# Selective scans of four directions on one core: a second buffer for x, one PSUM evacuation per projection, sums of y in column quarters, and more zero products on TensorE

## The chip, the cores and the metric

The kernel runs on one core of a Trainium2 chip. The metric is the device time of one execution in microseconds. The engines are named as the profile names them: PE is TensorE (matmuls), PEld its weight loads, DVE is VectorE, ACT is ScalarE, POOL is GpSimd, and SP is the queue that issues most DMAs.

## What is computed

A network of four layers on four images of 64 x 64 tokens with 96 channels. Layers 0 and 1 each run a selective scan in four directions over 4096 tokens, 192 inner channels and 16 states; layers 2 and 3 are an attention, a Fourier layer and feed-forward parts. The change lies in the scans, which both layers share:

```python
dts = jnp.einsum('bkrl,kdr->bkdl', dts, dt_projs_weight)
delta = jax.nn.softplus(dts + dt_projs_bias...)
def step(h, inp):
    dt, u, Bl, Cl = inp
    h = h * jnp.exp(dt[..., None] * A) + (dt * u)[..., None] * Bl[:, :, None, :]
    y = jnp.einsum('bkdn,bkn->bkd', h, Cl)
    return (h, y)
_, ys = jax.lax.scan(step, h0, (dt_t, u_t, B_t, C_t))
```

Layer 0's directions 0 and 1 follow the diagonals in a snake, 2 and 3 go by radius; layer 1's go along rows and columns, forwards and backwards. Afterwards the four results are put back in token order and added up.

## The kernel before

All is float32 in the scans. `Stream.run` (L1342) takes eight batches, one for each layer and image. Each is 4 directions x 4 segments of 1024 tokens, 16 segments in a row. Between two batches stands `side_by_side` (L748), which finishes the batch before (`merge`) and prepares the next image (`front`: input projection, convolution, x in token order in DRAM). Its small tiles (z_rows, xc, y_rows, yt, dx, halo) have buffers of their own.

**A segment** (`batch`, L1184) is 24 groups: 6 blocks of 32 channels (cb) by 4 blocks of 4 states (sg), so a group has 128 partitions (channel, state) and 1024 columns (tokens). For each group
- ACT makes the decay exp(dt*A) (`decay`, L1072),
- DVE makes t = u * B from PSUM (`enter`, L1076) and scans it (`recur`, L1083),
- POOL multiplies the states with C (`leave`, L1098), into a ring of three tiles hc,
- PE adds up the four states of each channel (`collect`, L1107): a product with the 128 x 32 matrix gather_y, summed in PSUM over the four groups of a channel block.

For each channel block PE first spreads dt*u over the states (`spread_u`, L1065) into the one PSUM tile u. DVE's order is fixed: enter, enter, recur, recur for each pair of groups. Two channel blocks make a pair: `collect` writes its 1024 tokens as two products of 512 columns, into two of the four 32-row quarters of the one PSUM bank y; once the pair is whole, `copy_y` (L1136) copies the bank, `turn` (L1148) transposes it, `keep_rows` (L1152) puts it into rows, and `store` (L1154) sends these to DRAM: for layer 0's directions 0 and 1 eight indirect scatters that POOL issues, otherwise one or two DMAs of SP.

**The next segment** is prepared meanwhile (`prepare`, L871): `turn_x` (L897) transposes its x, `keep_x` copies it to the one tile xs, `project` (L934) makes dt (192 channels, in two halves) and B and C for two halves of the tokens each, and `split` (L938) evacuates each projection: |dt + bias| and relu(dt + bias), with B and C in the first half. `low` (L986) and `log` work out softplus in four terms (with what exp loses in a low part), `add` (L1014) sums the terms on PE with the identity, `keep_dt` copies them, `times` (L1023) makes dt*u on POOL and so reads xs last. All PSUM steps but y, u and t share one bank, "m".

**The order** of all instructions of a batch is written by a planner, `Flow.run` (L136): each `Op` has an engine, a cost (`occ`), a latency to other engines, a due time and the operations it needs; "hard" ones (DVE, decay, leave, spread) may not be put off by others. Each engine works its queue in the order given. At each plan gap on PE, `keep_busy` (L1117) adds products with zeros (L1125: 96 x 32 zeros times 256 columns), which leave the sums as they are, but only where a group's sum is open in y:

```python
for _ in range(int((gap - 0.15) * 0.7 / 0.215)):
    self.nc.tensor.matmul(gr.seg.y[at : at + GC, :256], self.zeros, ..., start=False, stop=False, ...)
```

`self.open` is the last group collected, or None behind a block's fourth. The plan's costs are 0.87 for a collect, 1.75 for a spread, 0.88 and 0.87 for a product of `project` and `add`, 0.55 for `turn_x` and 0.5 for `turn`; a pair of groups takes 6.74 on DVE.

Of the kernel before, what the change touches and what calls it, by code (L numbers as in the profile page):

```python
# [113 lines left out]
class Op:  # L114


    def __init__(self, engine, occ, emit, deps=(), lat=0.15, due=None, hard=False, bank=0, after=0.0):
        self.engine, self.occ, self.emit, self.lat = engine, occ, emit, lat
        self.deps = [d for d in deps if d is not None]
        self.due, self.hard, self.bank, self.after = due, hard, bank, after  # L120
        self.users, self.left, self.seen = [], 0, 0.0


class Flow:
# [11 lines left out]
    def run(self):  # L136
# [22 lines left out]
        while left:  # L159
            best = None  # L160
            for engine, ops in ready.items():
# [7 lines left out]
                if strict and first:  # L169
                    limit = first[-1].due + drift - (3.2 if engine == "PE" else 0.5)  # L170
# [20 lines left out]
            if engine == "PE":  # L191
                self.fill(start - free[engine])
# [4 lines left out]
            free[engine] = start + op.occ  # L197
            done = start + op.occ
# [4 lines left out]
            for user in op.users:  # L203
                user.seen = max(user.seen, done if user.engine == engine else done + op.lat)
# [100 lines left out]
class Layer:  # L305


    def __init__(self, s, a, pre, x_in):
# [24 lines left out]
        self.bias_bc = None  # L333
        if self.ordered:
            self.bias_bc = k.t(w, [128, ND], pre + "dir_bc")
            nc.sync.dma_start(self.bias_bc[C:], a[pre + "dirBC"])
        conv_w = k.load(s.seg, a[pre + "conv_w"], "conv_w")
# [39 lines left out]
class Stream:  # L377
# [4 lines left out]
    def __init__(self, k, ctx, a, x, x1, y1):  # L382
# [20 lines left out]
        self.bc = k.t(w, [128, 2, NSG, SEG], "bc")  # L403
        self.zeros = k.t(w, [C, GC], "zeros")
        nc.gpsimd.memset(self.zeros, 0.0)

# [5 lines left out]
    def front(self, bt, plan, rings, first=None):  # L412
# [22 lines left out]
        def edges(s, st):  # L435

            halo = yield from take(self.tmp, [C, 2, HW], "halo", 2)
# [29 lines left out]
        def project(s, st):  # L467
# [31 lines left out]
            def outer(j):  # L499
# [6 lines left out]
                z = yield from take(self.tmp, [C, 2, CH], "z_rows", 2)  # L506
# [19 lines left out]
        def convolve(s, st):  # L526
            yield lambda: st.pad is not None
            xc = []
            for _ in range(C // GC):
                xc.append((yield from take(self.tmp, [128, CH], "xc", 3)))  # L530
# [26 lines left out]
            rows = yield from take(self.tmp, [128, 2, 4, DI], "y_rows", 1)  # L557
# [27 lines left out]
    def merge(self, bt, plan, rings):  # L585
# [29 lines left out]
        def times_d(n):  # L615

            x = yield from take(tmp, [128, T, DI], "dx", 1)
# [73 lines left out]
        def finish(n, acc, mv):  # L691
# [20 lines left out]
            yt = yield from take(tmp, [C, 2, CH], "yt", 1)  # L712
# [35 lines left out]
    def side_by_side(self, ahead, behind=None, flush=None, seg=None):  # L748
# [3 lines left out]
        plan, rings = Plan(), Rings(k)  # L752
        self.ended, self.idle = False, None
# [117 lines left out]
    def prepare(self, seg, base=0.0, before=None):  # L871
# [7 lines left out]
        def op(name, engine, occ, emit, deps=(), at=0.0, **kw):  # L879
            x = Op(engine, occ, emit, deps, due=base + at, **kw)  # L880
# [22 lines left out]
        def keep_x(j, parts):  # L903
            if (j, parts[0]) == (0, 0):
                seg.xs = k.t(self.seg, [C, 2, SEG], "xs")
# [9 lines left out]
        for j in range(0, SEG // 128, 2):  # L915
            here = [f for n, f in enumerate(seg.fetched) if len(seg.fetched) < 4 or seg.turned or n // 2 == j // 2]
            here.append(o.get(("X", j - 2)))
            if j == 0:
                here += [b.get(("u", h)) for h in range(2)]
# [18 lines left out]
        def split(half, j, what):  # L938
            if (half, j, what) == (0, 0, 0):
# [6 lines left out]
            if what == 0:  # L946
                nc.scalar.activation(v.z[:, half, cols], ps[:C], AF.Abs, bias=bias)  # L947
            elif what == 1:
                nc.scalar.activation(v.dt[:, half, cols], ps[:C], AF.Relu, bias=bias)
            elif lay.bias_bc is None:  # L950
                nc.scalar.copy(v.bc[:, cols], ps[C:])
            else:
                nc.scalar.activation(v.bc[:, cols], ps[C:], AF.Identity, bias=lay.bias_bc[C:, kd : kd + 1])

        last, chain = o["xs", SEG // 128 - 2], None
        for half in range(2):
            for j in range(2):
                at = 20.0 + 3.5 * (2 * half + j)
                free = []
                if (half, j) == (0, 0):  # L960
                    free = [b.get(n) for n in (("u", 0), ("u", 1), ("out", 0), ("out", 1), "bc_out", ("sum", 1, 1))]
# [13 lines left out]
                p = op(("z", half, j), "ACT", 0.6, partial(split, half, j, 0), [p], at=at + 2.0)  # L975
                if half == 0:
                    p = op(("z", half, j), "ACT", 0.63, partial(split, half, j, 2), [p], at=at + 3.0)
                op(("z", half, j), "ACT", 0.65, partial(split, half, j, 1), [p], at=at + 4.0, bank=-1)
# [7 lines left out]
        def low(half, what):  # L986
            if (half, what) == (0, 0):
                seg.dtu = k.t(self.seg, [C, 2, SEG], "dtu", bufs=2)
            z, r = v.z, seg.dtu
            if what == 0:  # L990
                nc.scalar.activation(z[:, half], z[:, half], AF.Exp, scale=-1.0)
            elif what == 1:
# [5 lines left out]
        for half in range(2):  # L998
            p = op(("low", half, 0), "ACT", 1.08, partial(low, half, 0), [o["z", half, 1], p], at=32.0 + 5.0 * half)
            p = op(("low", half, 1), "ACT", 1.08, partial(low, half, 1), [p], at=33.5 + 5.0 * half)  # L1000
            p = op(("low", half, 2), "ACT", 1.08, partial(low, half, 2), [p], at=35.0 + 5.0 * half)
# [6 lines left out]
        op("log", "ACT", 4.6, log, [o["low", 0, 2], o["low", 1, 2], b.get(("sum", 1, 1))], at=42.0)  # L1008
# [91 lines left out]
    def collect(self, gr):  # L1100

        nc, seg, cb = self.nc, gr.seg, gr.cb
        if gr.sg == 0 and cb % 2 == 0:
            seg.y = self.k.t(self.ps_y, [128, CH], "y")
        for part in range(2):
            at = (part * 2 + cb % 2) * GC
            nc.tensor.matmul(  # L1107
                seg.y[at : at + GC, :],
                self.gather_y,
                gr.hc[:, part * CH : (part + 1) * CH],  # L1110
# [4 lines left out]
        self.open = gr if gr.sg < NSG - 1 else None  # L1115

    def keep_busy(self, gap):  # L1117


        gr = self.open  # L1120
        if gr is None:
            return
        at = gr.cb % 2 * GC
        for _ in range(int((gap - 0.15) * 0.7 / 0.215)):
            self.nc.tensor.matmul(  # L1125
                gr.seg.y[at : at + GC, :256],
                self.zeros,
                gr.seg.bt.lay.diag.rearrange("p h t c -> p (h t c)")[:, :256],
                start=False,
                stop=False,  # L1130
# [1257 lines left out]
```

## Time and profile before

| | us |
|---|---|
| three runs | 15387.51, 15395.76, 15419.16 |
| median | 15395.76 |
| the profiled execution | 15402.95 |
| its span | 15401.2 |
| scan batches, first to last scan: layer 0 | 1350, 1331, 1338, 1326 |
| layer 1 | 1303, 1294, 1301, 1295 |
| between two batches | 99 to 225 |
| behind the last batch (layer 1's feed-forward, layers 2 and 3) | 3207 |
| granted TensorE clock, mean | 0.937 |

| engine | busy us | share of the span |
|---|---|---|
| PE | 13827.4 | 90% |
| DVE | 12827.4 | 83% |
| POOL | 9203.3 | 60% |
| ACT | 8327.7 | 54% |

| group of instructions | count | mean ns |
|---|---|---|
| recur, DVE L1083 | 3072 | 2355 and 2287 |
| enter, DVE L1076 | 3072 | 1239 |
| leave, POOL L1098 | 3072 | 2365 |
| dt*u, POOL L1023 | 256 | 2356 |
| decay, ACT L1072 | 3072 | 1151 |
| Abs and Relu in split, ACT L947, L949 | 512 each | 684, 679 |
| collect, PE L1107 | 12288 | 620 |
| zero products, PE L1125 | 7824 | 386 |

A matmul's duration runs to its modelled end, and matmuls overlap, so the time that one takes in the stream is the distance between starts. PE's 90% holds the zero products too. A product in float32 stands as two instructions.

### The profile page before, as it was taken

The numbers are of one execution on the slowest core, as the hardware profiler recorded it, in microseconds if no ns is written. First come the engines' busy times: TensorE is split into PE (matmuls) and PEld (weight loads), VectorE is DVE, ScalarE is ACT, GpSimd is POOL, SyncE is SP. The second block draws the span as 40 slices with busy tenths as digits, with TensorE's granted clock in tenths as the row PEclk, the third lists the DMA queues.
The fourth block names the chain that finished last, engine by engine and source line by source line (L and its number), as shares of the span: only waits on it lengthen the run. The fifth ranks groups of instructions, "written<-read, shape, count | busy, mean of one in ns | idle before, by whom it ended". The sixth has DMA issues, their size and how long they took to land. (4 is left out here: it accounts for less than half of the span.)

```text
span 15401.2 us, 196660 instructions
## 1 busy us (share of the span) xinstructions
PE 13827.4 (90%) x74369; PEld 5096.1 (33%) x74369; DVE 12827.4 (83%) x9642; ACT 8327.7 (54%) x13421; POOL 9203.3 (60%) x4657
## 2 busy tenths in 40 slices
PE   8899899989998999899989998999899789998877
PEld 3233333333333333333333333333233244443344
DVE  1999799978997899799979997999899856555655
ACT  3666466646664666466656665666566423232333
POOL 0788678867886688667747774777577620000123
PEclk9999899989998999899989999999999999998888
DMA  2333433343334333433343334333433400000122
GB/s 67 117 113 125 150 111 111 126 148 112 111 127 146 106 118 128 148 116 117 123 152 124 118 124 152 126 118 120 156 119 120 142 10 11 19 15 12 52 72 71
DMA packets 662768, 1637.49 MB, mean 106 GB/s; under 512 B 102822, under 2 KB 268460, under 8 KB 658045
## 3 DMA queue, kind: packets, MB, share of 16 engines
q1 hardware_dynamic: 624956, 1549.37, 31.4%
q0 software_dynamic: 36864, 75.55, 1.7%
q8 instruction: 588, 9.63, 0.3%
q14 instruction: 360, 2.94, 0.1%
HBM read 1295.03 MB, written 329.58 MB: 105 GB/s over the span
## 5 line engine op out<-in xcount | busy, mean ns | idle before, releaser
L1098 POOL TENSOR_TENSOR hc<-h,bc 128x1024 f32<-128x1024 f32 x3072 | 7198.4, 2365 | 2216.1 <-DVE h L1083 1909.0
L1083 DVE TENSOR_TENSOR_SCAN h<-da,state,t 128x1024 f32<-128x1024 f32 x2304 | 5300.4, 2355 | 26.0 <-ACT state L1094 16.3
L1072 ACT ACTIVATE da<-dts,L_A_logs 128x1024 f32<-128x1024 f32 x3072 | 3520.0, 1151 | 1832.2 <-DVE h L1083 1786.7
L1076 DVE TENSOR_TENSOR t<-u,bc 128x1024 f32<-128x1024 f32 x3072 | 3629.8, 1239 | 267.6 <-PE u L1065 193.5
L1107 PE MATMUL y<-hc,gather_y 128*32 128x512 f32 x12288 | 3529.1, 620 | 311.9 <-POOL hc L1098 241.7
L1125 PE MATMUL y<-L_diag,zeros 96*32 96x256 f32 x7824 | 1986.3, 386 | 0.0
L1083 DVE TENSOR_TENSOR_SCAN h<-da,t 128x1024 f32<-128x1024 f32 x768 | 1717.4, 2287 | 17.3 <-ACT da L1072 9.1
L1065 PE MATMUL u<-dtu,spread 32*128 32x512 f32 x3072 | 1573.1, 632 | 120.0 <-DVE t L1076 109.2
L1125 PEld LDWEIGHTS y<-L_diag,zeros 96*32 96x32 f32 x7824 | 852.8, 111 | 1425.0 <-issue 926.1
L1107 PEld LDWEIGHTS y<-hc,gather_y 128*32 128x32 f32 x12288 | 595.8, 109 | 2021.1 <-issue 1029.1
L934 PE MATMUL m<-xs,proj 96*128 96x512 f32 (+1 forms) x2048 | 1070.2, 641 | 67.3 <-ACT spare L1152 32.5
L1642 DVE SCALAR_TENSOR_TENSOR hcv<-padv,taps,hcv 128x2048 f32<-128x2048 f32 x384 | 902.2, 2350 | 13.4
L1566 POOL MEMSET padp<- 128x2448 f32 x32 | 68.6, 2143 | 1400.8 <-PE d L1606 1378.3
L1023 POOL TENSOR_TENSOR dtu<-dt,xs 96x1024 f32<-96x1024 f32 x256 | 603.0, 2356 | 506.1 <-ACT dt L1017 501.1
L1606 PE MATMUL d<-padp,diag 32*32 32x512 f32 x25600 | 885.7, 601 | 2.0 <-ACT hcp L1621 2.0
L1065 PEld LDWEIGHTS u<-dtu,spread 32*128 32x128 f32 x3072 | 521.4, 188 | 943.6 <-issue 588.0
L1017 ACT COPY dt<-m 96x512 f32<-96x512 f32 x512 | 297.2, 580 | 694.5 <-PE m L1014 690.0
L1014 PE MATMUL m<-dtu,ident 96*96 96x512 f32 x1024 | 563.8, 632 | 72.7 <-ACT dt L1017 65.9
L1606 PEld LDWEIGHTS d<-padp,diag 32*32 32x32 f32 x25600 | 484.4, 103 | 369.8 <-issue 196.9
L934 PEld LDWEIGHTS m<-xs,proj 96*128 96x128 f32 (+1 forms) x2048 | 324.6, 181 | 770.6 <-issue 483.8
L947 ACT ACTIVATE sp_z<-m,L_dtb 96x512 f32<-96x512 f32 x512 | 350.0, 684 | 409.5 <-PE m L934 393.5
L1014 PE MATMUL m<-sp_log,ident 96*96 96x512 f32 x1024 | 539.2, 608 | 0.0
(275 smaller groups left out, 15495.8 us busy)
## 6 DMA issues: line engine op xcount, KB each, us to landing
bc<-bc_dram SPq DMA_DIRECT2D x1024, 512.0 KB
dts<-dt_dram SPq DMA_DIRECT2D x768, 512.0 KB
dt_dram<-dt SPq DMA_DIRECT2D x256, 384.0 KB
y_tok<-spare SPq DMA_DIRECT2D x64, 768.0 KB
dt<-y_tok SPq DMA_DIRECT2D x128, 384.0 KB
x_tok<-y_rows SPq DMA_DIRECT2D x32, 768.0 KB
z_t<-z_rows SPq DMA_DIRECT2D x64, 384.0 KB
dx<-x_tok SPq DMA_DIRECT2D x64, 384.0 KB
```

The source lines that it names most:

```text
L934: nc.tensor.matmul(v.ps, seg.proj[:, src, to], seg.xs[:, src, chunks[j]], start=src == 0, stop=src == 1)
L1014: nc.tensor.matmul(v.ps, k.ident[:C, :C], term[:, half, chunks[j]], start=at == 0, stop=at == 3)
L1023: nc.gpsimd.tensor_mul(seg.dtu[:, half], v.dt[:, half], seg.xs[:, half])
L1065: self.nc.tensor.matmul(seg.u[:, cols], self.spread[rows, :], seg.dtu[rows, half, cols], start=True, stop=True)
L1072: self.nc.scalar.activation(gr.da, gr.seg.dts[gr.cb], AF.Exp, scale=scale)
L1076: self.nc.vector.tensor_mul(gr.t, gr.seg.u, self.bc[:, 0, gr.sg, :])
L1083: self.nc.vector.tensor_tensor_scan(gr.h[:, order], gr.da[:, order], gr.t[:, order], start, op0=ALU.mult, op1=ALU.add)
L1098: self.nc.gpsimd.tensor_mul(gr.hc, gr.h, self.bc[:, 1, gr.sg, :])
L1107: nc.tensor.matmul(seg.y[at : at + GC, :], self.gather_y, gr.hc[:, part * CH : (part + 1) * CH], start=gr.sg == 0, stop=gr.sg == NSG - 1, ...
L1125: self.nc.tensor.matmul(gr.seg.y[at : at + GC, :256], self.zeros, gr.seg.bt.lay.diag.rearrange("p h t c -> p (h t c)")[:, :256], start=Fal ...
L1606: nc.tensor.matmul(pc[i][j * 32 : (j + 1) * 32, :], diag[mine, ON_PE.index(t), tap, :], pad[mine, j * 8 + dy : j * 8 + dy + 8, dx : dx + H ...
L1642: nc.vector.scalar_tensor_tensor(to, win, wt, to, op0=ALU.mult, op1=ALU.add)
```

## The change

**xs.** There are two tiles for x: even segments use xs as before, odd ones the end of a new tile `area` of 7 x 1024 columns, from which the small tiles of `side_by_side` are now cut as well. `turn_x` needs the `times` of the segment before the last, no longer of the last.

**split.** Each projection is evacuated once, with its bias (Identity): in the first half dt, B and C together in 128 rows, in the second dt. `low` gains Abs and Relu over 1024 columns, from SBUF, so it has five steps a half instead of three; its first needs the sums of the segment before.

**collect.** The 1024 tokens go as four products of 256 columns, one into each 32-row quarter of y; the two channel blocks of a pair take the left and right half of the bank. The plan's cost is 0.46. `turn`, `keep_rows` (two copies) and `store` follow the new order, as does the table of scatter indices.

**Zero products.** `keep_busy` fills also behind a block's fourth group, in the half that opens next, and behind the copy of a pair, in the next tile y. Its share is 0.7 ahead of hard operations, 0.85 ahead of others.

**Planner.** Scatters are chained, each 3.0 behind the landing of the last; leave is counted as 1.2 later and the copy as 1.0 later for those that need them; the margin before a spread is 3.4 for 3.2; the dues of `prepare` are 8.0 later.

```diff
-                    limit = first[-1].due + drift - (3.2 if engine == "PE" else 0.5)
+                    limit = first[-1].due + drift - (3.4 if engine == "PE" else 0.5)
...
-                self.fill(start - free[engine])
+                self.fill(free[engine], start - free[engine], 0.7 if op.hard else 0.85)
...
-                user.seen = max(user.seen, done if user.engine == engine else done + op.lat)
+                near = user.engine == engine and not op.lands
+                user.seen = max(user.seen, done if near else done + op.lat + op.slack)
...
+        self.area = k.t(w, [128, 7 * SEG], "area")
...
-            x = Op(engine, occ, emit, deps, due=base + at, **kw)
+            x = Op(engine, occ, emit, deps, due=base + at + 8.0, **kw)
...
-                seg.xs = k.t(self.seg, [C, 2, SEG], "xs")
+                if seg.i % 2:
+                    seg.xs = self.area[:C, 5 * SEG :].rearrange("p (h t) -> p h t", h=2)
+                else:
+                    seg.xs = k.t(self.seg, [C, 2, SEG], "xs")
...
-                here += [b.get(("u", h)) for h in range(2)]
+                here += [before.before.o.get(("u", h)) for h in range(2)] if before and before.before else []
...
-            if what == 0:
-                nc.scalar.activation(v.z[:, half, cols], ps[:C], AF.Abs, bias=bias)
-            elif what == 1:
-                nc.scalar.activation(v.dt[:, half, cols], ps[:C], AF.Relu, bias=bias)
-            elif lay.bias_bc is None:
-                nc.scalar.copy(v.bc[:, cols], ps[C:])
+            if half == 0:
+                nc.scalar.activation(v.both[:, 0, cols], ps, AF.Identity, bias=lay.bias_bc[:, kd : kd + 1])
             else:
-                nc.scalar.activation(v.bc[:, cols], ps[C:], AF.Identity, bias=lay.bias_bc[C:, kd : kd + 1])
+                nc.scalar.activation(v.dt[:, 1, cols], ps, AF.Identity, bias=bias)
...
             if what == 0:
+                nc.scalar.activation(z[:, half], dt[:, half], AF.Abs)
+            elif what == 1:
                 nc.scalar.activation(z[:, half], z[:, half], AF.Exp, scale=-1.0)
-            elif what == 1:
+            elif what == 2:
+                nc.scalar.activation(dt[:, half], dt[:, half], AF.Relu)
+            elif what == 3:
                 nc.scalar.activation(r[:, half], z[:, half], AF.Identity, bias=1.0)
...
-            seg.y = self.k.t(self.ps_y, [128, CH], "y")
-        for part in range(2):
-            at = (part * 2 + cb % 2) * GC
+            seg.y = self.next_y or self.k.t(self.ps_y, [128, CH], "y")
+            self.next_y = self.vacant = None
+        for part in range(4):
+            at = part * GC
             nc.tensor.matmul(
-                seg.y[at : at + GC, :],
+                seg.y[at : at + GC, cb % 2 * 256 : (cb % 2 + 1) * 256],
                 self.gather_y,
-                gr.hc[:, part * CH : (part + 1) * CH],
+                gr.hc[:, part * 256 : (part + 1) * 256],
...
-        self.open = gr if gr.sg < NSG - 1 else None
+        self.open = None if gr.sg == NSG - 1 and cb % 2 else gr
...
-    def keep_busy(self, gap):
+    def keep_busy(self, now, gap, share):
-        gr = self.open
-        if gr is None:
+        lay = self.layers[0]
+        if self.open:
+            start = self.open.sg == NSG - 1
+            half = 1 if start else self.open.cb % 2
+            y = self.open.seg.y[:GC, half * 256 : (half + 1) * 256]
+        elif self.vacant and now > self.vacant.fin + 0.5:
+            if self.next_y is None:
+                self.next_y = self.k.t(self.ps_y, [128, CH], "y")
+            y, start = self.next_y[:GC, :256], True
+        else:
             return
-        at = gr.cb % 2 * GC
-        for _ in range(int((gap - 0.15) * 0.7 / 0.215)):
+        for _ in range(int((gap - 0.15) * share / 0.215)):
...
-            return [Op("POOL", 1.25, partial(scatter, j), lat=4.0) for j in range(SEG // 128)]
+            for j in range(SEG // 128):
+                ops.append(Op("POOL", 1.25, partial(scatter, j), ops[-1:], lat=3.0))
+                ops[-1].lands = True
+            return ops
...
+                    g2.leave.slack = 1.2
...
-                        0.87,
+                        0.46,
                         partial(self.collect, g2),
```

## The prediction

> **What bounds the kernel now.** I read the windows of the eight scan batches first, then who waits for whom, then the timeline of TensorE inside one batch. The windows run from the first to the last scan of a batch, two of layer 0 and one of layer 1 here (columns: length, then busy us and count of PE, PEld, DVE, ACT and POOL, granted clock, DMA share, GB/s):
>
> ```profile
> 386.00:1736.00 1350.00, 1245.75 (x4070) 406.85 (x4070) 1291.53 (x768) 854.04 (x1498) 1097.32 (x543) 0.95 0.35 116
> 5054.00:6380.00 1326.00, 1225.71 (x4069) 400.69 (x4068) 1290.48 (x768) 849.20 (x1447) 1097.47 (x544) 0.97 0.35 116
> 8050.00:9344.00 1294.00, 1209.43 (x4104) 398.08 (x4102) 1288.14 (x768) 841.67 (x1215) 970.76 (x415) 0.99 0.37 119
> ...
> sum 10538.00, PE 9799.81 PEld 3218.18 DVE 10320.10 ACT 6745.20 POOL 8268.85; mean PE 1224.98 PEld 402.27 DVE 1290.01 ACT 843.15 POOL 1033.61
> ```
>
> VectorE sets the pace: 10320.1 of 10538 us. The other 217.9 us (1.4% of the span) are all that a change of the scans can win without shortening VectorE's own work, which the diff leaves as it is; 181 of them lie in layer 0. The waits of one layer-0 batch say where:
>
> ```profile
> DVE t L1076 <- PE u L1065: 40.7, 24, 5.4
> DVE h L1083 <- ACT state L1094: 5.0, 3, 2.1
> DVE h L1083 <- ACT da L1072: 2.6, 2, 2.0
> ```
>
> VectorE waits for the spread of dt*u (L1065), that is, for TensorE's queue. What is late ahead of TensorE shows on POOL in one such stall:
>
> ```profile
> 2313.53 1.00 POOL L1162 DMA_INDIRECT y_tok<-spare,scan_idx  x1 [1.31 <-DMA y_tok<-spare,scan_idx]
> 2317.64 0.97 POOL L1162 DMA_INDIRECT y_tok<-spare,scan_idx  x1 [3.10 <-issue]
> 2318.64 4.67 POOL L1098 TENSOR_TENSOR hc<-h,bc 128x1024 f32<-128x1024 f32 x2
> ```
>
> The second scatter holds POOL's queue until the first has landed, the products behind it (L1098) come late, and so do the collects on TensorE. In layer 1, without scatters, VectorE loses 6 to 13 us in a batch. There TensorE's queue looks like this:
>
> ```profile
> 7024.25 1.02 PE L1107 MATMUL y<-hc,gather_y 128*32 128x512 f32 x3
> 7025.11 1.68 PE L1125 MATMUL y<-L_diag,zeros 96*32 96x256 f32 x7
> ...
> 7030.45 1.02 PE L1014 MATMUL m<-sp_log,ident 96*96 96x512 f32 x2
> 7031.40 1.05 PE L1107 MATMUL y<-hc,gather_y 128*32 128x512 f32 x4
> 7032.28 1.03 PE L1125 MATMUL y<-L_diag,zeros 96*32 96x256 f32 x4
> 7033.24 1.98 PE L1065 MATMUL u<-dtu,spread 32*128 32x512 f32 x4
> 7035.15 0.66 PE L1148 MATMUL m<-ident,yc 128*128 128x128 f32 x4
> ```
>
> A float32 product is two instructions. 512 columns take 0.43 us each in the stream ((31.40-30.45)/2, less the change of form), a zero product's 256 columns 0.215 us each (four in 1.03, less the 0.38 of the last), thus 0.43 us for one zero product. `keep_busy` counts it as 0.215. A collect's four instructions take 0.88 us (31.40 to 32.28): its two column groups run side by side. A change of form between narrow and full products costs 0.08 to 0.1 us each way.
>
> **TensorE's budget for one segment** (80.9 us: 24 groups of VectorE at 6.74 us a pair). Counting instructions in the window 8050:9344: spread 24, projection 16 and sums 32 of 0.43 = 31.0 us; transposes 28 of 0.11 = 3.1; collects 24 x 0.86 = 20.6; zeros 61 x 0.215 = 13.2; idle stretches between the ends of one stream and the next start, worked out from the starts in the trace, 5.9 us in pieces under 0.13 (changes of form) and 6.5 in longer ones. Sum 80.3. TensorE has 6.5 us to give.
>
> **The change, part by part.**
>
> Collects in quarters: eight instructions of 256 columns in four groups, where four of 512 in two groups were. If four groups run side by side as two do now, a collect is 0.43 us: 24 x 0.43 = 10.3 us of TensorE freed. No row here has a 128-row product in four groups; the bounds are 0.43 (full overlap) and 0.86 (none beyond two); I take 0.43, since the convolution's 32x32 tiles overlap far more: in the window 9466:9500 its 216 products of 512 columns (L542) keep TensorE busy for 10.99 us, and at 0.43 each would be 92. The Trainium skill's "TensorE: Matmul & The Clock Gate", Measured speedup, gives 2.38x for three column tiles, not 3x; in its proportion a collect would be about 0.54 us, an estimate, and the freed time 7.7 us.
>
> Zero products: today they stand only where a group's sum is open. The plan's own gaps follow from its costs: 80.9 - (24 x 0.87 + 6 x 1.75 + 16 x 0.87 + 8 x 0.88 + 4 x 0.55 + 3 x 0.5) = 24.8 us, and with collects at 0.46, 34.7 us. After the change all are filled but those between a pair's last collect and half a microsecond behind its copy, three of some 2 us: 28 to 30 us remain, about 6 of them before spreads (share 0.7), the rest at 0.85. For a gap g the count is the whole part of (g - 0.15) x 0.85 / 0.215, so 3.95 a microsecond, and at 0.43 us each that is 1.7 us of work for 1 us of gap, less 0.26 for the 0.15 and 0.21 on average for the fraction. Over n gaps: 1.7 x 23 + 1.4 x 6 - 0.47n = 47.5 - 0.47n. Today there are 17 runs of zeros and 10 unfilled stretches in a segment, so n is 25 to 35: 31 to 36 us; a longer plan of unfilled time takes 2 off. I take 34 us, that is 79 products (158 instructions) where 31 (61) stand now. The same formula with 0.7 and the open gaps alone (13 to 15 us) gives the 30 products that the trace has, so it counts right.
>
> TensorE then needs 31.0 + 3.1 + 10.3 + 5.9 + 34 = 84.3 us, and about 0.7 more for changes of form at new runs and for a first wait in each chain: 85 us for 80.9. Ends: 31 us of zeros and no extra, 81.3; 37 us and 7 of changes of form, 88.4; collects at 0.86 add 10 to either, which I leave out of my own range. Above 80.9 nothing hides it: TensorE runs in order, spreads come later by the excess, and VectorE, which has no slack, waits.
>
> The clock: a starved TensorE gets slow. At 2310 us spread instructions start 0.85 us apart instead of 0.43, and the granted clock is 0.95 to 0.97 in layer 0 against 0.98 to 0.99 in layer 1. The Trainium skill's "TensorE: Matmul & The Clock Gate", Why this matters for your kernels, asks for no idle of more than some 3 us, which speaks for the zeros; by that rule alone the layer-0 waits shrink, by the budget the queue is overfull. The gain of a full clock is inside the 218 us.
>
> Scatters: each now waits in the plan 3.0 us for the one before (`lands`), so POOL's products no longer stand behind them. POOL's waits for landings are 123.5 us in all (four batches); at most those 124 us of the 181 come back, at least none; VectorE waits for the same spreads either way.
>
> One evacuation per projection: ACT loses 4 Abs (0.684), 4 Relu (0.679) and 2 copies (0.63), 6.7 us, gains 4 Identity of 0.68 and, on 1024 columns of SBUF, 2 Abs and 2 Relu of 1.06: 7.0 us. Even; ACT is 65% busy in a batch. The bank "m" is free some 1.3 us earlier in each of four projections, the chain behind it 4 us longer: nothing, hidden by its lead: in the layer-1 segment that starts at 8212 us the first product dt*u (L1023) ends 24 us before the next segment's first spread, in the layer-0 one at 2274 us 6 us. Uncovered, 0.3 us of ACT a segment would be 38 us in all. Two copies of rows (0.37 each, as L566's 256 columns) for one of 0.58: 0.16 x 3, hidden on ACT too.
>
> Two x buffers: turn_x no longer waits for the products of the segment before (u, L1023); the chain may begin up to 10 us sooner, while its dues are 8 us later. Worth 0 to 57 us, the rest of layer 0's 181. The store's rows of two tokens make DMA pieces of 1.5 KB for 3 KB; DMA engines are 36% busy: nothing. The later collects (slack 1.2) move gaps, not their sum.
>
> **Sum.** 16 segments at 85 us are 1360 us; a batch now takes 10538 / 8 = 1317: +43 x 8 = +344 us, the gains of layer 0 swallowed, since a full queue cannot catch up. The profiled execution took 15402.95 us (span 15401.2 and 1.8 around it), 7 us over the median of 15395.76. So 15403 + 344 = 15747, less 7: **15740 us**. Its own range: 82.5 to 88 us a segment, 15396 - 10538 + 128 x T, gives 15418 to 16122.
>
> **Rivals.** (1) TensorE fits. If the zeros stay under 30.5 us a segment (71 products, so under some 18,200 instructions in all against 7824), the queue keeps up, spreads come on time, the clock stays up and scatters no longer stall POOL. Of 218 us some 40 remain (batch starts and state copies), less some new lateness: -100 to -190, **15250 us**. For it: 10.3 us freed, and the count depends on how the plan cuts its gaps; 40 gaps would give 29 us. Against it: the formula above, at 1.7 us of work for 1 us of gap. (2) It evens out: 30 to 32 us of zeros, scatters' gain of 100 us eaten by late spreads in layer 1: **15400 us**. (3) The idle zeros block: they write the next y and so wait for the copy of the last one (ACT, L1136, 0.58 us, now released by PE y); the spread stands behind. 384 pairs x 0.58 = 223 us, less 100 won: **15520 us**. Against: half a microsecond is left free behind the copy.
>
> **Chances.** Forecast 0.54, rival 1 0.34, rival 2 0.07, rival 3 0.05. A measurement of this kernel tells 0.2% (31 us) from no change. Faster 0.34, same 0.07, slower 0.59. The range takes in most of rival 1 and stops within the forecast's upper end: 15230 to 16050.
>
> **What would show it.** Right: L1125's line has 19,000 to 21,000 instructions; TensorE never waits inside a batch, VectorE waits 3 to 6 us a segment for u in layer 1 too, where it now waits under 1; granted clock 1.0 there. Collects: eight instructions within 0.5 us. Wrong: fewer than 18,200 zeros, layer-1 batches still of 1294 us, and layer-0 batches of 1300 to 1320; then the gain is the scatters' and the clock's. Scatter waits on landings should be near 0 either way.

## The result and the profile after

| | us | ratio to before |
|---|---|---|
| before, four runs beside it | 15407.46 (15387.51 to 15429.38) | |
| after, four runs | 16916.4 (16876.13 to 16931.46) | 1.0975 (95%: 1.0948 to 1.1002) |
| after, span of the profiled execution | 16874.3 | |

The change makes the kernel 9.75% slower: 1509 us, where 344 were forecast, and the time lies above the range.

First the windows from the first to the last scan of a batch, after the change, one of layer 0 and one of layer 1 (length; busy us and count of PE, PEld, DVE, ACT, POOL; granted clock; DMA share; GB/s), and the sum over all eight:

```profile
5429.00:6900.00 1471.00, 1439.30 (x7383) 599.38 (x7383) 1297.28 (x768) 840.50 (x1461) 1100.31 (x543) 0.98 0.32 105
...
8800.00:10340.00 1540.00, 1471.95 (x7325) 604.37 (x7325) 1298.26 (x768) 833.99 (x1230) 973.05 (x415) 0.95 0.32 100
...
sum 12046.00, PE 11641.36 PEld 4825.28 DVE 10382.73 ACT 6685.03 POOL 8289.64; mean PE 1455.17 PEld 603.16 DVE 1297.84 ACT 835.63 POOL 1036.20
```

VectorE's own work has hardly moved (10382.7 us against 10320.1), but the batches are 1508 us longer in sum: the whole loss lies in the scans, and VectorE now stands idle for 1663 us of them instead of 218. Layer 1, where little was late before, lost most: 1540 us instead of 1294. What VectorE waits for in these two windows:

```profile
DVE t L1109 <- PE u L1098: 173.3, 77, 8.7
DVE h L1116 <- ACT state L1127: 1.3, 3, 0.7
```

```profile
DVE t L1109 <- PE u L1098: 247.8, 94, 9.0
```

The spread again (L1098, once L1065), 10.8 and 15.5 us a segment. The groups of TensorE's products, over the whole execution (count, then busy us and mean ns of one, then the idle time before them):

```profile
L1166 PE MATMUL y<-L_diag,zeros 96*32 96x256 f32 x22128 | 5287.8, 386 | 0.5 <-ACT yc L1177 0.5
L1141 PE MATMUL y<-hc,gather_y 128*32 128x256 f32 x24576 | 2207.5, 398 | 0.0
L1189 PE MATMUL m<-ident,yc 128*128 128x128 f32 x1536 | 286.8, 311 | 274.6 <-ACT dt L978 110.9 <-ACT yc L1177 52.5 <-ACT dt L1050 43.9
```

22128 zero instructions stand where 7824 stood, 173 a segment. They do not wait for the copy of y (0.5 us in all). The turn (L1189), however, waits 274.6 us. Before, it waited 43.6:

```profile
L1148 PE MATMUL m<-ident,yc 128*128 128x128 f32 x1536 | 284.5, 309 | 43.6 <-ACT yc L1136 43.6
```

How this looks on TensorE, in layer 1:

```profile
9231.83 0.64 PE L1141 MATMUL y<-hc,gather_y 128*32 128x256 f32 x8
9232.28 2.32 PE L1166 MATMUL y<-L_diag,zeros 96*32 96x256 f32 x10
9234.54 1.12 PE L963 MATMUL m<-xs,proj 96*128 96x512 f32 x2
9235.59 2.35 PE L1166 MATMUL y<-L_diag,zeros 96*32 96x256 f32 x10
9237.87 1.98 PE L1098 MATMUL u<-dtu,spread 32*128 32x512 f32 x4
...
9247.74 1.10 PE L963 MATMUL m<-xs,proj 96*96 96x512 f32 x2
9250.38 0.66 PE L1189 MATMUL m<-ident,yc 128*128 128x128 f32 x4 [1.53 <-ACT dt L978]
9250.96 1.48 PE L1166 MATMUL y<-L_diag,zeros 96*32 96x256 f32 x6
9252.38 1.98 PE L1098 MATMUL u<-dtu,spread 32*128 32x512 f32 x4
```

A collect's eight instructions take 0.45 us (9231.83 to 9232.28), as forecast. Twenty zero instructions stand ahead of the spread at 9237.87, without a gap. VectorE's enter, which needs that spread, shows what it cost:

```profile
9239.89 2.36 DVE L1109 TENSOR_TENSOR t<-u,bc 128x1024 f32<-128x1024 f32 x2 [3.43 <-PE u L1098]
```

Then comes what the forecast left out: the turn at 9250.38 stands 1.53 us, because the bank "m" that it needs is still being evacuated by ACT (L978), and the next zeros and the next spread, behind it in the queue, come later too. (The new evacuation is not needed for such waits: in e14 below, which has the old one, the turn waits 240.7 us.)

On POOL the scatters behave as forecast: they wait 2.0 us in all for the landing of another, in 4 places, for 123.5 us in 60 places before. A stretch with one:

```profile
5559.77 1.00 POOL L1205 DMA_INDIRECT y_tok<-spare,scan_idx  x1 [0.16 <-issue]
5561.66 2.35 POOL L1131 TENSOR_TENSOR hc<-h,bc 128x1024 f32<-128x1024 f32 x1 [0.90 <-DVE h L1116]
5565.83 2.36 POOL L1131 TENSOR_TENSOR hc<-h,bc 128x1024 f32<-128x1024 f32 x1 [1.81 <-PE y L1141]
```

Now the products behind them wait for PE instead (their ring hc is freed by late collects): 1718.3 us in all, for 108.0 before.

### The profile page after: what moved, and what is told of

It reads as the page before. It is cut to its first block, busy times and chain, and to the rows that moved or that the text cites. A ratio compares the mean times of both kernels' runs of the same rounds, so it can differ in the third digit from the quotient of the medians.

```text
span 16874.3 us, 249857 instructions
## 1 busy us (share of the span) xinstructions
PE 15646.2 (93%) x100961; PEld 6705.1 (40%) x100961; DVE 12900.8 (76%) x9645; ACT 8267.9 (49%) x13549; POOL 9206.3 (55%) x4657
## 5 line engine op out<-in xcount | busy, mean ns | idle before, releaser
L1131 POOL TENSOR_TENSOR hc<-h,bc 128x1024 f32<-128x1024 f32 x3072 | 7214.1, 2360 | 3683.5 <-PE y L1141 1718.3
L1166 PE MATMUL y<-L_diag,zeros 96*32 96x256 f32 x22128 | 5287.8, 386 | 0.5 <-ACT yc L1177 0.5
L1166 PEld LDWEIGHTS y<-L_diag,zeros 96*32 96x32 f32 x22128 | 2360.0, 111 | 2759.3 <-issue 692.2
L1141 PE MATMUL y<-hc,gather_y 128*32 128x256 f32 x24576 | 2207.5, 398 | 0.0
L1098 PE MATMUL u<-dtu,spread 32*128 32x512 f32 x3072 | 1599.4, 641 | 39.2 <-DVE t L1109 34.5
L1141 PEld LDWEIGHTS y<-hc,gather_y 128*32 128x32 f32 x24576 | 733.7, 110 | 1441.2 <-issue 956.8
L1050 ACT COPY dt<-m 96x512 f32<-96x512 f32 x512 | 297.4, 581 | 1678.5 <-PE m L1047 1678.3
L1098 PEld LDWEIGHTS u<-dtu,spread 32*128 32x128 f32 x3072 | 530.6, 192 | 782.4 <-issue 658.2
L1177 ACT COPY yc<-y 128x512 f32<-128x512 f32 x384 | 224.4, 584 | 1055.9 <-PE y L1141 1054.7
L1056 POOL TENSOR_TENSOR dtu<-dt,xs 96x1024 f32<-96x1024 f32 x128 | 301.7, 2357 | 502.0 <-ACT dt L1050 501.9
L963 PE MATMUL m<-area,proj 96*128 96x512 f32 (+1 forms) x1024 | 549.1, 653 | 11.2 <-ACT dt L976 5.2
L963 PE MATMUL m<-xs,proj 96*128 96x512 f32 (+1 forms) x1024 | 541.3, 645 | 15.9 <-ACT xs L937 8.0
L1189 PE MATMUL m<-ident,yc 128*128 128x128 f32 x1536 | 286.8, 311 | 274.6 <-ACT dt L978 110.9
```

What stands on the lines that cost most here:

```text
L963: nc.tensor.matmul(v.ps, seg.proj[:, src, to], seg.xs[:, src, chunks[j]], start=src == 0, stop=src == 1)
L1056: nc.gpsimd.tensor_mul(seg.dtu[:, half], v.dt[:, half], seg.xs[:, half])
L1098: self.nc.tensor.matmul(seg.u[:, cols], self.spread[rows, :], seg.dtu[rows, half, cols], start=True, stop=True)
L1131: self.nc.gpsimd.tensor_mul(gr.hc, gr.h, self.bc[:, 1, gr.sg, :])
L1141: nc.tensor.matmul(seg.y[at : at + GC, cb % 2 * 256 : (cb % 2 + 1) * 256], self.gather_y, gr.hc[:, part * 256 : (part + 1) * 256], start=g ...
L1166: self.nc.tensor.matmul(y, self.zeros, lay.diag.rearrange("p h t c -> p (h t c)")[:, :256], start=start, stop=start, tile_position=(0, 0),)
```

## The experiments

The median of the kernel before was 15263 to 15407 us from one occasion to the next, so each kernel is compared by its ratio to the kernel before as measured beside it. A number without an interval is one run.

| run | edit | ratio (95%) | zero products | clock |
|---|---|---|---|---|
| e3 | after, no zeros in the scans | 1.023 | 0 | 0.77 |
| e1 | after, zeros counted at 0.43 | 1.0150 (1.0126 to 1.0174) | 4901 | 0.875 |
| e2 | after, zeros where a sum is open, share 0.7 | 1.0149 (1.0127 to 1.0171) | 4884 | 0.876 |
| e8 | after, share 0.5 | 1.0071 (1.0051 to 1.0090) | 6478 | 0.918 |
| e5 | after, share 0.6 | 1.0325 (1.0295 to 1.0356) | 8091 | 0.927 |
| after | shares 0.7 and 0.85 | 1.0975 (1.0948 to 1.1002) | 11064 | 0.942 |
| e15 | after, old planner numbers | 1.1033 (1.1014 to 1.1052) | 11758 | 0.954 |
| e4 | before, twice the zeros | 1.094 | 8914 | 0.963 |
| e7 | before, scatters chained | 0.9930 (0.9907 to 0.9953) | 4052 | 0.944 |
| e17 | e7, share 0.8 for 0.7 | 0.9978 (0.9968 to 0.9988) | 5055 | 0.951 |
| e9 | e7, one evacuation | 0.9935 (0.9919 to 0.9952) | 3550 | 0.933 |
| e10 | e7, two x | 0.9987 (0.9978 to 0.9997) | 3895 | 0.937 |
| e12 | e7, planner numbers | 1.0077 (1.0060 to 1.0094) | 2866 | 0.899 |
| e16 | e12, share 1.0 | 1.0042 (1.0026 to 1.0058) | 4279 | 0.927 |
| e13 | e7, dues 4 earlier | 1.0040 (1.0026 to 1.0053) | 3183 | 0.921 |
| e6 | after without quarters and new zeros | 1.0056 (1.0034 to 1.0077) | 3517 | 0.909 |
| e11 | e7, quarters, share 0.5 in all gaps | 0.9955 (0.9939 to 0.9972) | 6667 | 0.938 |
| e14 | e11, shares 0.7 and 0.85 | 1.0945 (1.0923 to 1.0967) | 11717 | 0.960 |

(Runs are named by the first part of their labels. Clock: the mean granted over the whole span. A product is two instructions. Before has 3912 products at 0.937.)

**Too many zeros, or something else?** First the count alone.

```diff
-        for _ in range(int((gap - 0.15) * share / 0.215)):
+        for _ in range(int((gap - 0.15) * share / 0.43)):
```

> The kernel after, with a zero product counted at 0.43 us instead of 0.215 in the number that fills a gap; where gaps are filled stays as changed. 4901 zero products instead of 11064 (38 a segment, 16.5 us instead of 37.2). If TensorE is overfull (my theory), it needs 44.2 + 5.9 + 16.5 = 66.6 us of each 80.9 and the batches fall to 1295-1315 us: 15200 to 15350 us. If the other edits (x buffers, the longer chain on ACT, quarters) make the time, it stays above 16500. If zeros behind a pair's copy block the queue, 384 pairs x 0.58 us stay: 15450 to 15600.

```diff
+        share = 0.7
+        if self.open and self.open.sg == NSG - 1:
+            return
...
-        elif self.vacant and now > self.vacant.fin + 0.5:
+        elif False:
```

> The kernel after, with zero products only where a group's sum is open, at the share 0.7, as in the kernel before: 4884 products, as many as in the run with the half count, but in other gaps. Overfull TensorE: within 60 us of that run, 15220 to 15380. If zeros in gaps with no open sum block the queue behind the copy, this one is 150 to 250 us faster than that run. If the other edits make the time, above 16500.

```diff
     def keep_busy(self, now, gap, share):
+        return
```

> The kernel after without any zero product in the scans. Overfull TensorE: far below the kernel after, since 37 us a segment are gone; but TensorE may be granted a lower clock: at half clock its 44 us of work become 88 and with 6 of changes of form 94 (17000 us); at a mean of 0.8 some 61 us, 15250 to 15500. I expect 15300 to 15800 and a granted clock below 0.9 in the batches. If the other edits make the time, above 16500 with VectorE waiting for spreads as now.

And the kernel before, with the opposite edit:

```diff
-        for _ in range(int((gap - 0.15) * 0.7 / 0.215)):
+        for _ in range(int((gap - 0.15) * 1.4 / 0.215)):
```

> The kernel before with the share 1.4 for 0.7, nothing else: 8914 zero products instead of 3912 (70 a segment, 29.9 us). Overfull TensorE: 54.7 + 5.9 + 29.9 = 90.5 us a segment, 16440 us, and up to 16900 with waits; VectorE waits for u in every segment. If the zeros are harmless, 15400.

Doubling the share of zeros (8914 products for 3912) makes the kernel before nearly as slow as the change does: 1.094. Its windows, layer 0 and layer 1:

```profile
5367.00:6859.00 1492.00, 1449.36 (x5260) 528.52 (x5261) 1296.31 (x768) 844.54 (x1447) 1097.73 (x544) 0.99 0.32 103
8694.00:10206.00 1512.00, 1473.70 (x5391) 537.56 (x5392) 1299.68 (x768) 839.58 (x1215) 971.63 (x415) 1.00 0.32 102
```

So an overfull TensorE is enough by itself, at a full clock, without any other part of the change. But with fewer zeros the changed kernel does not become fast either: 1.015 in e1 and e2 (15506 and 15473 us, where 15200 to 15380 were expected), 1.023 without any. Without zeros, TensorE is busy for less, and the clock falls to 0.71 to 0.74 (the same two kinds of window; then one of layer 1 in e1, for the clock of 0.87):

```profile
5041.00:6415.00 1374.00, 1121.23 (x4651) 364.25 (x4650) 1291.87 (x768) 842.44 (x1462) 1097.88 (x544) 0.73 0.35 112
8102.00:9467.00 1365.00, 1152.50 (x4654) 377.39 (x4656) 1291.58 (x768) 833.91 (x1230) 971.27 (x416) 0.71 0.35 113
```

```profile
8018.00:9368.00 1350.00, 1249.79 (x5846) 462.17 (x5848) 1292.17 (x768) 836.78 (x1230) 972.25 (x416) 0.87 0.36 114
```

The Trainium skill's "TensorE: Matmul & The Clock Gate", Why this matters for your kernels, asks for no idle of more than some 3 us; these runs agree with its direction, as the mean clock of a batch goes from 0.72 through 0.87 (38 products a segment) to 0.98 (86, layer 0). None of them shows the 3 us.

**Is there a share that pays?** The share was set to 0.5 and 0.6 for all gaps.

> The same with a share of 0.5: 6478 products, 51 a segment, 21.8 us, 71.9 us of 80.9. Cold clock: between the run with the half count (1.015) and the one with 0.6, some 0.995 to 1.008. Other edits: 1.01 to 1.02.

> The kernel after with one share of 0.6 for all gaps (0.215 as changed): 8091 zero products, 63 a segment, 27.2 us, so TensorE needs 44.2 + 5.9 + 27.2 = 77.3 us of 80.9. The half count left TensorE at 66.6 us and at a granted clock of 0.87 in the batches, and lost 1.5% against the kernel before. If that was the cold clock, this run comes back to 0.985 to 1.000 of the kernel before, with a clock of 0.96 or more. If the other edits cost the 1.5%, it stays at 1.01 to 1.02 in spite of the clock.

1.007 and 1.0325; the second is above what either reading of e5 expected. At 0.6 the zeros are 63 products, 27.2 us a segment, well under the 30.5 us to which rival 1 let TensorE fit, and layer 1 is already at 1394 to 1410 us a batch, layer 0 at 1340 to 1368:

```profile
5054.00:6411.00 1357.00, 1307.52 (x6665) 524.17 (x6664) 1293.83 (x768) 843.12 (x1462) 1099.77 (x544) 0.96 0.35 113
8172.00:9583.00 1411.00, 1338.84 (x6663) 532.38 (x6661) 1296.45 (x768) 837.33 (x1231) 973.30 (x416) 0.94 0.35 109
```

So the changed kernel loses time earlier than the budget said, and even the best share tried leaves it behind the one before. That is not the amount of work on TensorE alone: e17 below has as much in a segment (71.5 us for the 71.1 of e5) and is at 0.9978. Another part of the change costs time.

**The other parts.** e6 is the change with the collects and zeros of before; e7 is the kernel before with this alone:

```diff
-            return [Op("POOL", 1.25, partial(scatter, j), lat=4.0) for j in range(SEG // 128)]
+            for j in range(SEG // 128):
+                ops.append(Op("POOL", 1.25, partial(scatter, j), ops[-1:], lat=3.0))
+                ops[-1].lands = True
+            return ops
```

> The kernel before with all of the change but the quarters and the zero products: two x buffers, one evacuation per projection, chained scatters, the planner's slack and dues; collects of two halves and zeros only where a group's sum is open at 0.7 (3517 products). If these edits are harmless or help, 0.985 to 1.000 of the kernel before; if they cost the 1.5%, 1.01 to 1.02, with TensorE waiting for ACT's evacuation ahead of the transposes (L1189, some 60 us a batch).

> The kernel before with the chained scatters alone. POOL's waits for landings (123.5 us in the kernel before) go to near 0; of the 181 us that VectorE waits in layer 0's batches up to 124 come back: 0.992 to 0.998. If POOL's lateness was not what delayed the spreads, 1.000.

The scatters alone win 0.70%. Their layer-0 window of the fourth batch:

```profile
4934.00:6236.00 1302.00, 1227.73 (x4139) 405.60 (x4138) 1289.08 (x768) 848.40 (x1447) 1097.97 (x543) 0.98 0.36 118
```

1302 us for the 1326 of before; the eight batches sum to 10432 for 10535. With the rest on top (e6), the gain becomes a loss of 0.56%. So the rest was put on e7 one at a time: the new `split` and `low` (e9), the tile `area` and the second xs (e10), and the planner's numbers (e12):

```diff
-                    limit = first[-1].due + drift - (3.2 if engine == "PE" else 0.5)
+                    limit = first[-1].due + drift - (3.4 if engine == "PE" else 0.5)
...
-            x = Op(engine, occ, emit, deps, due=base + at, **kw)
+            x = Op(engine, occ, emit, deps, due=base + at + 8.0, **kw)
...
+                    g2.leave.slack = 1.2
...
+        copied.slack = 1.0
```

> The kernel before with the chained scatters (which alone gave 0.993) and, on top, one evacuation per projection with its five-step `low`; no second x buffer, no planner changes, no quarters, zeros as before. All of these together without quarters (the run with the rest only) gave 1.0056, so 1.26% lies between. Theory (the planner's dues, 8 us later, push the sums of softplus into the last spreads of a segment): the evacuation costs little, 0.993 to 0.997. Rival (the chain from projection to dt*u is some 4 us longer, so dtu and the sums come late): 1.000 to 1.006, with VectorE's waits for u near 250 us instead of 115.

> The kernel before with the chained scatters and, on top, the second x buffer alone (area shared with the small tiles between batches). Theory: nothing, 0.991 to 0.995, since x was never late. Rival (the chain gains up to 57 us, as the prediction allowed): 0.989 or less. Second rival (x turned too early takes bank m and TensorE's slots from the sums, or the shared area holds back the work between batches): over 0.997, and then the gaps between batches or the waits for u say which.

> The kernel before with the chained scatters and, on top, the planner's numbers alone: dues of prepare 8 later, leave 1.2 and the copy 1.0 later for those that need them, margin before a spread 3.4. Theory: this is most of the 1.26% between the scatters alone (0.993) and the rest only (1.0056): 1.000 to 1.005, with VectorE waiting for u near the last spreads of a segment (waits for u 200 to 300 us instead of 115). Rival (they cost nothing): 0.991 to 0.996.

The evacuation costs nothing that these runs can tell (0.9935). The second x costs 0.6%, all in layer 0 (batches 1350, 1325, 1321, 1320 for e7's 1316, 1308, 1300, 1302; layer 1 stays within 1294 to 1309 in both): VectorE's wait for u in the fourth batch, in e10 and then in e7:

```profile
DVE t L1103 <- PE u L1092: 29.0, 13, 6.4
```

```profile
DVE t L1077 <- PE u L1066: 12.9, 9, 3.1
```

The planner's numbers cost 1.5%, a little more than expected. Singly the three parts cost 0.05, 0.6 and 1.5% on e7; together, in e6, they cost 1.3%, so they don't add up. VectorE's waits for u in all, in e12 and then in e7:

```profile
DVE t L1077 <- PE u L1066: 338.3, 181, 8.0
```

```profile
DVE t L1077 <- PE u L1066: 115.4, 78, 7.0
```

Sorted by channel block, 265.5 us of those of e12 stand ahead of the sixth and last block of a segment, and 1.0 us of those of e7. So the spread that comes late is the last one of a segment, as the expectation had it. Which of the four numbers makes it late was not tried. The four numbers also leave fewer zeros in the plan (2866 products for 4052) and a colder clock; the layer-1 window of e12:

```profile
8031.00:9365.00 1334.00, 1238.78 (x3703) 375.69 (x3704) 1290.77 (x768) 825.62 (x1215) 971.49 (x416) 0.89 0.36 115
```

e16 puts zeros back (share 1.0) to tell the clock from the lateness, e13 moves the dues the other way:

```diff
-            x = Op(engine, occ, emit, deps, due=base + at, **kw)
+            x = Op(engine, occ, emit, deps, due=base + at - 4.0, **kw)
```

> The run with the planner's numbers alone (1.0077, 2866 zero products, granted clock 0.90 to 0.92 in the batches) with the share of zero products 1.0 instead of 0.7, so that some 4,100 to 4,400 products stand in them, as in the run with the scatters alone (4052, clock 0.97 to 0.98, 0.993). Theory (the dues cost by way of the clock: they shift the plan's gaps to where no sum is open, fewer zeros stand there, TensorE's clock falls): clock 0.96 to 0.98 and 0.993 to 0.998. Rival (the sums themselves come too late for the last spreads): the clock rises, the time stays at 1.005 to 1.012.

> The kernel before with the chained scatters and the dues of prepare 4 earlier instead of 8 later. If the lead of the sums over the last spreads is what the dues cost (8 later: from 0.993 to 1.0077), then 4 earlier takes away some of the 115 us that VectorE still waits for u: 0.986 to 0.991. Rival (there is lead enough already at the old dues): 0.992 to 0.995. Second rival (x then comes too early, and its turns stand in TensorE's queue waiting for the fetch or the bank): over 0.996.

In e16 the layer-1 window has a clock of 0.94, and is 11 us shorter (second line; the first is of layer 0):

```profile
5043.00:6378.00 1335.00, 1279.28 (x4304) 430.56 (x4303) 1290.88 (x768) 844.99 (x1447) 1098.87 (x543) 0.96 0.35 115
8058.00:9381.00 1323.00, 1247.66 (x4008) 400.34 (x4008) 1290.55 (x768) 831.84 (x1216) 972.49 (x416) 0.94 0.36 116
```

1.0042, between the theory's range and the rival's: as many zeros as in e7 (4279 for 4052) give back only a quarter of the 1.5%, so their number is not the main cause. In layer 0 e16 even has more of them than e7 (1182 to 1227 instructions a batch for 1018 to 1024), and its batches there are still 1334 to 1352 us for 1300 to 1316. Of its 276.5 us of waits for u, 198.5 stand ahead of the sixth block. So the last spread stays late with the zeros back; but the clock did not come back to e7's 0.98 either, and how much of the rest the clock makes stays open. Dues 4 earlier lose as well (1.004, again with fewer zeros, 3183). Neither direction is a gain; the expectation of one was wrong.

**Quarters and zeros without the rest.** e11 is e7 with the quarters and one share of 0.5 in all gaps, e14 the same with the change's own shares; e15 is the whole change with the old planner numbers.

> The kernel before with the chained scatters and the quarters (cost 0.46), zeros in all gaps with the one share 0.5; old x, old evacuation, old planner numbers. Theory: TensorE's load is then as in the run with share 0.5 (1.007) and its other edits' 1.26% are gone: 0.990 to 0.997, no better than the scatters alone, because the freed 10 us of collects must be filled again for the clock. Rival 1 (the quarters do free TensorE for good): 0.985 or less. Rival 2 (zeros in the gaps where no sum is open hurt by themselves, by their wait for the copy of y): 1.002 or more.

> As the run with quarters and share 0.5 (0.9955), but with the change's own shares 0.7 and 0.85; old x, old evacuation, old planner numbers. Theory (zeros and the planner's dues hurt each for itself; dues 1.5%): the zeros are 36 to 38 us a segment again and the time is that of the change less some 1.5%: 1.07 to 1.09. Rival (most of the excess over the budget comes from the chain behind the later dues, whose waits an overfull queue multiplies): 1.02 to 1.05.

> The whole change with the planner's numbers put back (dues, leave, copy and margin as before). Theory: 1.07 to 1.09, within 1% of the run with quarters and full shares alone, since x and the evacuation cost only some 0.6%. Rival (the dues don't matter once TensorE is overfull): 1.09 to 1.10, as the change itself.

e11 is at 0.9955, no better than the scatters alone. e14 is at 1.0945. Their layer-1 windows, e11 first:

```profile
7903.00:9209.00 1306.00, 1227.69 (x6320) 474.00 (x6318) 1289.10 (x768) 834.81 (x1262) 972.12 (x416) 0.98 0.36 118
```

```profile
8728.00:10225.00 1497.00, 1459.07 (x7536) 609.77 (x7536) 1296.88 (x768) 828.42 (x1263) 970.22 (x415) 0.99 0.33 103
```

The only difference is the share. So the number of zeros makes the loss by itself. Once TensorE is overfull, the planner's numbers show no cost of their own: without them e15 is at 1.1033, no faster than the change, though it has more zeros (11758). The theory's 1.07 to 1.09 was wrong for both, if by little for e14; for e15 the rival's 1.09 to 1.10 was nearer.

**The last question**, whether the kernel with chained scatters wants more zeros:

```diff
-        for _ in range(int((gap - 0.15) * 0.7 / 0.215)):
+        for _ in range(int((gap - 0.15) * 0.8 / 0.215)):
```

> The kernel before with the chained scatters (0.993 at share 0.7, 4052 zero products) and share 0.8: some 4,600 to 4,900 products, 2 to 3 us of TensorE more in a segment. Theory (the budget of 80.3 us of 80.9 is full but for 6.5 us of idle, 51 to 54 us of other work and more than 27 us of zeros and collects over 10.3 don't fit): 0.992 to 1.000, no gain, as the waits that a faster clock saves come back as queue. Rival (the clock still has something to give): 0.985 to 0.991.

0.9978: clock 0.98 to 0.99 in all batches, and yet slower than e7 by half a percent. Every batch of layer 1 is at 1312 to 1316 us; one of them:

```profile
7931.00:9247.00 1316.00, 1262.31 (x4392) 427.38 (x4392) 1291.81 (x768) 839.31 (x1215) 971.44 (x416) 0.99 0.36 117
```

VectorE waits for u 221 times, for 78 in e7 (186.0 us for 115.4).

## Why the forecast was right in its direction and wrong in its size

The trace gives an account of TensorE's stream. In a window of 16 segments each instruction is given its distance at full clock (0.215 us for a zero, 0.43 for 512 columns, 0.11 for a transpose, 0.43 for a quartered and 0.86 for a halved collect). What a run of like instructions takes beyond that, until the next run begins, is a change of form where it is under 0.25 us, and a wait or a slow stretch where it is longer. In us per segment:

| kernel, layer | zeros | all work | changes of form | waits, slow | segment |
|---|---|---|---|---|---|
| before, 1 | 13.2 | 67.6 | 5.0 | 8.1 | 80.8 |
| e7, 0 | 13.7 | 68.1 | 4.7 | 8.5 | 81.4 |
| e17, 1 | 17.0 | 71.5 | 4.8 | 5.9 | 82.2 |
| e11, 1 | 22.3 | 66.5 | 5.4 | 9.7 | 81.6 |
| e5, 0 | 27.0 | 71.1 | 4.1 | 9.5 | 84.7 |
| e5, 1 | 26.9 | 71.1 | 3.9 | 13.1 | 88.1 |
| e14, 1 | 38.9 | 83.1 | 3.6 | 6.9 | 93.5 |
| e4, 1 | 30.5 | 84.9 | 4.9 | 4.6 | 94.5 |
| after, 0 | 37.0 | 81.1 | 4.4 | 6.5 | 91.9 |
| after, 1 | 36.2 | 80.3 | 4.2 | 11.8 | 96.2 |

**The step that failed** is the sum of TensorE's need: 84.3 us "and about 0.7 more for changes of form at new runs and for a first wait in each chain". The mechanism was right (an overfull TensorE makes the spreads late, and VectorE waits); two terms were too small. The zeros were put at 34 us and are 37.0 and 36.2: +3.0 and +2.2. All that is not stream, 5.9 + 0.7 = 6.6 in the forecast, is 10.9 in layer 0 and 16.0 in layer 1: +4.3 and +9.4. The rest of the work is 44.1 for 44.4. Together +7.0 and +11.3 a segment; the segments took 91.9 and 96.2 instead of 85. With 64 segments in each layer, 64 x 6.9 + 64 x 11.2 = 1158 us; 344 + 1158 = 1502, and 1509 were measured. (The segments are measured, so this agreement only says that the loss lies in the batches; what divides it is the table.)

The error lay in treating TensorE's longer idle stretches, 6.5 us in the budget, as time that it "has to give". An overfull queue does not close them: e4, e14 and e17, all at a clock of 0.99 or 1.0, still show 9.5 to 10.7 us of changes of form and waits. The profile names what TensorE waits for in only part of this: 2.3 us a segment in e14 and 2.4 in e4, for evacuations of "m" and copies of y; what the rest of the longer stretches are was not told apart. So some 70 to 71 us of instructions fit into the 80.9 (an estimate: 80.9 less 9.5 to 10.7), not 74 (80.9 less 6.6): e17, with 71.5, is already over, at 82.2. In the changed kernel less than that fits: e5, with 71.1, has 13.6 and 17.0 us of changes of form and waits. Where the last 5.5 us of layer 1 come from is only partly told apart: with the old x, evacuation and planner (e14) that layer has 10.5, with the new x and evacuation but the old planner (e15) 13.7, with all 16.0 (and 17.0 in e5, under fewer zeros). In the window of layer 1 shown, TensorE's wait at the turn for the evacuation of L978 is 25.5 us in 11 places, and for the copies of L1050 11.3 in 9.

**By the other steps:**
- *VectorE sets the pace, and at most 218 us (1.4%) can be won:* right; no version won more than 0.7%.
- *Collects in quarters take 0.43 us:* right, 0.45 with the change to the next form. But the 10 us that they free were no gain in any run: e11, which fills them with zeros, is no faster than e7, and e2, with quarters and more zeros than before (4884 for 3912), has a clock of 0.87 to 0.90 in its batches, where before has 0.95 to 0.99. (e2 holds the planner's numbers too, with which e12 has 0.89 to 0.92.)
- *One zero product is 0.43 us, counted as 0.215:* right, and e14 against e11 shows that the number of zeros alone makes the loss. The count of 19,000 to 21,000 instructions was low (22128).
- *VectorE 3 to 6 us late a segment, TensorE never waiting, clock 1.0:* wrong in the same way: 10.8 and 15.5 us, waits in both layers, clock 0.98 and 0.95.
- *Scatters, at most 124 us:* right: the batches of e7 are 103 us shorter in sum.
- *One evacuation costs nothing:* right (e9). The lead of 6 us given for layer 0 is misread: in that batch the first product dt*u ends 21.3 to 25.7 us ahead of the next segment's first spread, as in layer 1.
- *Two x buffers, 0 to 57 us of gain:* wrong in sign: e10's batches are 99 us longer in sum than e7's. Why x costs this in layer 0 wasn't tried further.
- *Later dues and slack "move gaps, not their sum":* wrong: 1.5% on a kernel that otherwise keeps pace, with the waits ahead of a segment's last spread.
- *Rival 1 (TensorE fits, 15250):* its price was wrong as well as its bound. At 22.4 us of zeros, with the old planner numbers, x and evacuation (e11), TensorE fits, and 0.45% is gained, no more than from the scatters alone; at 27.2 us in the changed kernel (e5) it doesn't.
- *Rival 3 (idle zeros block behind the copy):* did not happen; 0.5 us in all.

The fastest version measured is the kernel before with the chained scatters alone: 15281.72 us (15258.38 to 15297.01) beside 15386.06 for before, 0.9930 (0.9907 to 0.9953); e9's 0.9935 can't be told from it.

## What to carry to other kernels

Price a filler instruction by the distance of its starts in the trace before its count is raised: here a product of two instructions was counted as one, and filling "85% of a gap" put 1.7 us of work into 1 us. An engine's idle time in the middle of a chain is not all room: here the fastest kernel leaves 13 of 81 us of TensorE to changes of form and waits (e7), and the next fill tried, with 10.7 (e17), is slower at a better clock. And where one part of a bundle is easy to isolate (the scatters), run it alone: it was worth 0.7%, and the bundle buried it.

## What the runs showed of the hardware

- Products of 128 rows by 32 columns in four column groups of 256 float32 columns run fully side by side: eight instructions start within 0.45 us, where one group's two would take 0.43. The estimate of 0.54 us from the Trainium skill's "TensorE: Matmul & The Clock Gate", Measured speedup vs the span model (2.38x for three tiles), was too high here.
- The granted clock, as a mean over a batch, rises with the fill of the queue by degrees: 0.71 to 0.74 with no zeros (44.2 us of work in 85.3), 0.89 at 62.3 in 83.4 (e12), 0.94 at 66.4 in 82.7 (e16), 0.98 to 1.0 from 68 in 81 up (e7, e17, e4, e14). The amount does not set it alone: e11, with zeros in all gaps, has 0.98 at 66.5 in 81.6, while after, layer 1, has 0.95 at 80.3 in 96.2 and e5, layer 1, 0.94 at 71.1 in 88.1. These two have the longest waits of the table (11.8 and 13.1 us), part of which the slower clock itself makes (80.3 us of work at 0.95 would be 84.5, an estimate).
- The changed kernel without zeros, at a clock of 0.71 to 0.74, is 2.3% slower than the kernel before; its planner numbers, which cost 1.5% by themselves on e7, are in that, so the clock's own share is not told apart. An overfull queue costs 9 to 10% (e4, e14, e15, after).
